# Narrow 0/1 rows of a graph kernel made tile by tile from one source, in rows with gaps

## The chip, the cores and the metric

The kernel runs on one core of a Trainium2 chip. The metric is the device time of one execution in microseconds. Before the change three runs took 2859.52, 2863.18 and 2864.38 us; the median is 2863.18.

The engines are named as in the profile: PE (TensorE, with PEld for its weight loads), DVE (VectorE), ACT (ScalarE), POOL (GpSimd, which here issues the indirect gathers) and SP (which issues most of the other DMAs).

## What is computed

Two graph layers, a last product, a residual and a layer norm, over 12,500 nodes with 256 features and 200,000 edges. `dst` is sorted, and drawn so that small node numbers get many more edges.

```python
def _sage_conv(x, src, dst, W_l, b_l, W_r):
    msgs = x[src]
    agg = jax.ops.segment_sum(msgs, dst, num_segments=N_NODES)
    deg = jax.ops.segment_sum(jnp.ones((src.shape[0],), x.dtype), dst, num_segments=N_NODES)
    mean = agg / jnp.maximum(deg, 1.0)[:, None]
    return mean @ W_l + b_l + x @ W_r
...
h = jax.nn.relu(_sage_conv(x, src, dst, W1_l, b1, W1_r))
h = jax.nn.relu(_sage_conv(h, src, dst, W2_l, b2, W2_r))
return h @ W3 + b3
...
x = _layernorm(x + _L0_gnn_ref(...), axis=-1)
```

## The kernel before

The edges are cut into 1563 tiles of 128. The aggregation is made in two ways, side by side.

**Cold nodes** (few edges each) are gathered. One round takes four tiles: POOL issues four indirect DMAs (`got`, L251), each of which brings 128 rows of `x` or `h`. DVE makes the 0/1 matrix `one` (`select`, L208), PE multiplies it with the rows into `part_ps` (L263), ACT copies this to `some` (L273), DVE makes a second 0/1 matrix `two` (L214: 128 lanes compared with one number per partition, written in f32), PE multiplies again into `sum_ps` (L279, L285), and DVE adds that to a ring of sums (L293) and degrees (L289). There are four `got` buffers, so a gather of round i + 4 needs the products of round i to be done.

**Hot nodes** (the first 5 blocks of 256 nodes in layer 1, 7 in layer 2) are counted. For every block `count` (L669) goes through its tiles of edges and makes, for each tile, the 0/1 rows `pick` (L684: 5, 7 or 9 times 98 elements wide, f16 in, bf16 out), `low` (L688: 128 wide) and, from tile 128 on, `aft` (L694: 98 wide). `low` and `aft` are made for four tiles in one instruction, from two sources that are both spread over the tiles. PE multiplies `low` with `pick` and the `low` of the tile before with its `aft` into `count_ps` (L716 while a tile is below 128, L727 and L731 from there). ACT (L733), or DVE below tile 128 (L720), puts the result into the count matrix of the block. `product` (L645 to L666) then multiplies the counts with all rows of `x` or `h`, which were split into three bf16 parts before (`split_rows`, L640: DVE's `rest` and `parts`, L635 and L636; SP stores them). In layer 2 the counts of four blocks are loaded again instead of made.

Each finished block of 128 nodes goes through `first_block` or `last_block`: the products with W_l and W_r (`sage`, L882 and L887), and DVE's and ACT's work on them.

**What orders the work.** PE's and POOL's orders are as written in the program; the other engines' orders are chosen by a scheduler. `layer` (L576) goes round by round: it issues the next round of gathers, then fills in as much of the counting, products and splits as a table of costs says is due for this round (`count_cost` and its neighbours, L757 to L764), with pieces of finished blocks between. So PE works off a fixed mixture, in which the gathers' products stand between the counting and the dense products. Layer 1 has six stages: the count of block 0 beside the splits, and then the count of the next block beside the product of the one before. Layer 2 follows, with the count of the last block only. Inside `count`, `pick` runs one tile ahead:

```python
for t in range(lo_g, highs[g]):
    for u in (t, t + 1):
        if u < highs[g] and u not in ahead:
            ahead[u] = pick(u)
    r, s, aft = ahead.pop(t)
```

There are three `pick` buffers, and two of `low` and `aft` with four tiles each. The weights of both layers are loaded at the start over ACT's queue (`weight`, L541) into tiles of their own.

Of the kernel before, what the change touches and what calls it, by code (L numbers as in the profile page):

```python
# [7 lines left out]
F32 = mybir.dt.float32  # L8
F16 = mybir.dt.float16
# [14 lines left out]
P = 128  # L24
# [25 lines left out]
def by_runs(  # L50
# [86 lines left out]
    lo_t2 = consts.tile([P, P], BF16, name="lo_t2")  # L137
    lo2 = consts.tile([P, len(groups)], F32, name="lo2")
    place = consts.tile([1, len(groups)], I32, name="place")
    low_t = consts.tile([P, HC * P], BF16, name="low_t")  # L140
    spans = [(lows[g] // P, -(-highs[g] // P)) for g in range(HG)]
    tiles_of = [highs[g] - lows[g] for g in range(HG)]
    key_t = [consts.tile([P, n], F32, name=f"key_t{g}") for g, n in enumerate(tiles_of)]
    after_t = [consts.tile([P, n], F16, name=f"after_t{g}") for g, n in enumerate(tiles_of)]
    offs = [consts.tile([1, n], I32, name=f"offs{g}") for g, n in enumerate(tiles_of)]

    ident = consts.tile([P, P], F32, name="ident")
    lane_b = consts.tile([P, P], BF16, name="lane_b")
    steps = consts.tile([P, WIDEST * NB], F16, name="steps")
    ones = consts.tile([P, 1], F32, name="ones")  # L150
    ones_b = consts.tile([P, 1], BF16, name="ones_b")
    zeros_b = consts.tile([P, P], BF16, name="zeros_b")
# [49 lines left out]
    def select(g, r, second):  # L202

        t0, n = groups[g]
        lo, c0 = (lo_t2, C2) if second and t0 // P == C2 else (lo_t, C0)
        a = t0 - c0 * P + r
        one = chosen_pool.tile([P, G, W], F32, name="one", bufs=AHEAD + 1)
        nc.vector.tensor_tensor(  # L208
            one, lo[:, a:a + n * (G - 1) + 1:n].unsqueeze(2).to_broadcast([P, G, W]),
            lane_b[:, :W].unsqueeze(1).to_broadcast([P, G, W]), op=OP.is_equal)  # L210
        if r < n - 1:
            return one, None
        two = chosen_pool.tile([P, P], F32, name="two", bufs=AHEAD + 2)
        nc.vector.tensor_scalar(two, lane_b, lo2[:, g:g + 1], None, op0=OP.is_equal)  # L214
        return one, two

    def left_after(g):

# [76 lines left out]
    with tc.tile_pool(name="setup", bufs=1) as su, \  # L295
# [58 lines left out]
                       allow_small_or_imprecise_dtypes=True)  # L354
        nc.vector.tensor_scalar(ident, diff, 0.0, None, op0=OP.is_equal)
        nc.vector.tensor_copy(lane_b, lane)


        def columns(t, cs, to, name, t0=0, a=None, b=None):
# [178 lines left out]
                                       accum_out=test(1))  # L538


    def weight(w, name):  # L541
        t = consts.tile([P, NC, w.shape[1]], F32, name=name)
        nc.scalar.dma_start(t, w.rearrange("(c p) f -> p c f", p=P))
        return t

    w1l_sb, w1r_sb = weight(w1l, "w1l_sb"), weight(w1r, "w1r_sb")
    w2l_sb, w2r_sb, w3_sb = weight(w2l, "w2l_sb"), weight(w2r, "w2r_sb"), weight(w3, "w3_sb")

    biases = consts.tile([P, 3, D], F32, name="biases")
    for i, b in enumerate((b1, b2, b3)):  # L550
# [25 lines left out]
    def layer(gathers, block, n_pieces, dense, dense_cost):  # L576


        queue, waiting, done = [], [], set()
        turn = 0  # L580

        def begin():
            if waiting and len(queue) < MOST:
                b, *of = waiting.pop(0)
                p = block(b, *of)
                next(p)
                queue.append([b, p, n_pieces - 1, turn + APART])

        def pieces():


            nonlocal turn
            turn += 1
            q = next((q for q in queue if q[3] <= turn), None)
            if q:
                next(q[1])
                q[2:] = q[2] - 1, turn + APART
                if q[2] == 0:
                    done.add(q[0])
                    queue.remove(q)  # L600
            begin()

        filler = dense(waiting)
        spent = 0.0

        def fill(upto):
            nonlocal spent
            while spent < upto:
                spent += next(filler, 1e9)

        i0, n = gathers.i, len(gathers.rounds)
        begun = gathers.hot // P
        for i in range(i0, n + 1):
            before = gathers.step()
            due = dense_cost * min(1.0, (i + 1 - i0) / (n - i0 - 8))
            for part in range(3):
                if part == 2 and before:
                    gathers.summed(*before, done)
                    while begun < left_after(before[0]):
                        waiting.append((begun,))  # L620
                        begun += 1
                pieces()
                fill(spent + (due - spent) / (3 - part))
        fill(1e8)
        while queue or waiting:
            pieces()
# [42 lines left out]
    def count(g, to):  # L669

        lo_g = lows[g]
        off_dve = Values(offs[g], lo_g, DVE, DN)
        off_act = Values(offs[g], lo_g, ACT, DN)
        n_pick = 0
        ahead = {}
        fours = {}

        def pick(t):
            nonlocal n_pick
            w = room(t)  # L680
            i = n_pick % len(picks)
            r = picks[i]
            n_pick += 1
            nc.vector.tensor_scalar(r[:, :w * NB], steps[:, :w * NB],  # L684
                                    key_t[g][:, t - lo_g:t - lo_g + 1], None, op0=OP.is_equal)
            if t % G == 0:
                low = work.tile([P, G, P], BF16, name="low")
                nc.vector.tensor_tensor(  # L688
                    low, low_t[:, t:t + G].unsqueeze(2).to_broadcast([P, G, P]),
                    lane_b.unsqueeze(1).to_broadcast([P, G, P]), op=OP.is_equal)  # L690
                aft = None
                if t + G >= FIRST:
                    aft = work.tile([P, G, NB], BF16, name="aft")
                    nc.vector.tensor_tensor(  # L694
                        aft, after_t[g][:, t - lo_g:t - lo_g + G].unsqueeze(2).to_broadcast([P, G, NB]),
                        steps[:, :NB].unsqueeze(1).to_broadcast([P, G, NB]), op=OP.is_equal)
                fours[t // G] = low, aft
            low, aft = fours[t // G]
            return r, low[:, t % G], None if aft is None else aft[:, t % G]

        before = None
        for t in range(lo_g, highs[g]):
# [4 lines that stand above are left out]
            w = room(t)  # L707

            halves = [(a, min(a + 5, w)) for a in range(0, w, 5)]
            if t < FIRST:  # L710
                j = t % G
                if j == 0:
                    ps = count_pool.tile([P, 1024], F32, name="count_ps")
                    c = ps[:, 512 - 5 * NB:][:, :w * NB]
                for a, b in halves:
                    nc.tensor.matmul(c[:, a * NB:b * NB], lhsT=s, rhs=r[:, a * NB:b * NB],  # L716
                                     start=j == 0, stop=j == G - 1)
                if j == G - 1:
                    into = to[:, :, bass.ds(off_dve.at(t - j), w)]
                    nc.vector.tensor_tensor(into, into, c.rearrange("p (d s) -> p s d", s=NB), op=OP.add)  # L720
                yield count_cost(t)
            else:
                ps = count_pool.tile([P, 1024], F32, name="count_ps")
                c = ps[:, 512 - 5 * NB:][:, :w * NB]
                for a, b in halves:
                    alone = a > 0 or before is None
                    nc.tensor.matmul(c[:, a * NB:b * NB], lhsT=s, rhs=r[:, a * NB:b * NB],  # L727
                                     start=True, stop=alone)
                    if not alone:

                        nc.tensor.matmul(c[:, :NB], lhsT=before[0], rhs=before[1],  # L731
                                         start=False, stop=True)
                nc.scalar.copy(to[:, :, bass.ds(off_act.at(t), w)], c.rearrange("p (d s) -> p s d", s=NB))  # L733
                yield count_cost(t)
            before = s, aft
            if t == FIRST - 1:

                most = work.tile([P, 1], F32, name="most", bufs=1)
                nc.vector.tensor_reduce(most, to[:, :, :NEAR], axis=mybir.AxisListType.XY, op=OP.max)
                nc.vector.tensor_scalar(test(), most, 256.0, None, op0=OP.is_ge)  # L740
# [231 lines left out]
        layer(gathers_1, first_block, 3, staged(stages_1), cost_of(stages_1))  # L972
    block_pool = ctx.enter_context(tc.tile_pool(name="block_ps", bufs=2, space=PSUM))
    count_pool = ctx.enter_context(tc.tile_pool(name="count_ps", bufs=1, space=PSUM))
    layer(Gathers(h_d, True), last_block, 5, staged(stages_2), cost_of(stages_2))


# [377 lines left out]
```

## Time and profile before

| | |
|---|---|
| median of three runs | 2863.18 us |
| the profiled execution | 2859.81 us |
| its span | 2858.0 us |
| mean granted TensorE clock | 0.92 |
| PE's busy share, by fortieths | `3465768978988998999985777878888898999995` |
| POOL's | `5777887777777777777775777777777777777771` |
| DVE's | `6688775654554565665563124443323343444443` |
| the chain that ended last | PE 45%, DMA 21%, POOL 10%, "issue" 6%, DVE 3%, ACT 2% |

The rows by fortieths give the busy tenths of 71 us each. The gathers of layer 1 run from 24.7 to 1520.6 us and those of layer 2 from 1545.0 on; the step between them can be seen as the 5 in PE's and POOL's rows. In the groups, "xcount | busy, mean ns | idle before" stands behind the names; the releaser behind an idle time says what came last. "issue" means that nothing in the profile was waited for.

### The profile page before, as it was taken

The page shows a single profiled execution, that of the slowest core. Times are in us where ns is not written, and L with a number is a line of the kernel's source. Part 1 is how long each engine was busy: PE and PEld are TensorE (multiplying, and loading weights), DVE is VectorE, ACT ScalarE, POOL GpSimd, SP SyncE. Part 2 cuts the span into 40 slices and gives each one's busy share as a digit, 9 for nine tenths or more (in the row PEclk, how much of TensorE's full clock was granted, in tenths as well). Part 3 has the DMA queues.
Part 4 walks back from the last instruction along what each step waited for, and adds up shares of the span by engine and source line. Part 5 has one row for each costly group of instructions (what it writes and reads, how often), then busy time and mean ns, then how long its engine had stood idle before and what let it go on. Part 6 is the DMA issues. An engine that isn't in the chain of part 4 may idle for free.

```text
span 2858.0 us, 53490 instructions
## 1 busy us (share of the span) xinstructions
PE 2327.7 (81%) x18268; PEld 1602.2 (56%) x18268; DVE 1455.2 (51%) x4334; ACT 1098.8 (38%) x2270; POOL 2092.5 (73%) x2074
## 2 busy tenths in 40 slices
PE   3465768978988998999985777878888898999995
PEld 1122325655755666766764455556566666777773
DVE  6688775654554565665563124443323343444443
ACT  0432765654554564565562013333111122222222
POOL 5777887777777777777775777777777777777771
PEclk9777668999988999999998999899999999999998
DMA  4466669768868869867864777677889889888872
GB/s 124 141 201 208 186 194 304 244 203 284 271 202 283 272 209 306 261 204 246 264 187 146 232 247 223 217 221 242 282 289 304 288 284 305 281 270 267 271 245 64
DMA packets 420974, 676.49 MB, mean 237 GB/s; under 512 B 72419, under 2 KB 279385, under 8 KB 420697
## 3 DMA queue, kind: packets, MB, share of 16 engines
q1 hardware_dynamic: 316263, 400.60, 42.8%
q0 software_dynamic: 99072, 270.66, 30.7%
q8 instruction: 150, 2.46, 0.3%
q10 hardware_dynamic: 5362, 1.72, 0.3%
q14 instruction: 127, 1.04, 0.1%
HBM read 582.84 MB, written 89.92 MB: 235 GB/s over the span
## 4 chain that ended last, share of the span: by engine, by line
PE 45%; DMA 21%; POOL 10%; issue 6%; DVE 3%; ACT 2%; DVEq 0%; SPq 0%; ACTq 0%; POOLq 0%
PE dense_ps L659 17%; POOL got L251 10%; PE part_ps L263 6%; PE block_ps L882 5%; DMA rows<-x_d 5%; DMA rows<-h_d 5%; PE block_ps L887 4%; DMA got<-h_d,src_t 4%; PE count_ps L727 4%; DMA x_sb<-in_x_dram 4%; DMA got<-in_x_dram,src_t 3%; PE sum_ps L279 3%; PE block_ps L954 2%; PE block_ps L859 2%; ACT counts L733 1%
## 5 line engine op out<-in xcount | busy, mean ns | idle before, releaser
L251 POOL DMA_INDIRECT got<-in_x_dram,src_t x1076 | 1143.7, 1063 | 374.1 <-issue 286.6
L251 POOL DMA_INDIRECT got<-h_d,src_t x988 | 946.7, 958 | 336.0 <-issue 261.0
L659 PE MATMUL dense_ps<-counts,rows 128*128 128x256 bf16 x7056 | 951.2, 277 | 86.2 <-DMA rows<-h_d 47.7
L659 PEld LDWEIGHTS <-rows 128*128 128x128 bf16 x7056 | 670.0, 99 | 307.6 <-issue 84.8
L733 ACT CAST counts<-count_ps 128x686 f32 (+2 forms) x620 | 540.3, 872 | 263.5 <-PE count_ps L727 193.3
L263 PE MATMUL part_ps<-got,one 128*32 128x257 f32 (+1 forms) x4128 | 364.5, 427 | 225.0 <-DMA got<-h_d,src_t 107.5
L684 DVE TENSOR_SCALAR pick<-steps,key_t 128x686 bf16<-128x686 f16 (+2 forms) x748 | 300.0, 411 | 134.4 <-PE count_ps L727 114.8
L727 PE MATMUL count_ps<-pick,low 128*128 128x490 bf16 (+2 forms) x1052 | 324.4, 362 | 47.3 <-ACT counts L733 25.9
L208 DVE TENSOR_TENSOR one<-lo_t,lane_b 128x128 f32<-128x128 bf16 x516 | 148.2, 287 | 346.3 <-PE part_ps L263 342.3
L273 ACT COPY some<-part_ps 128x257 f32<-128x257 f32 (+1 forms) x361 | 134.5, 373 | 427.0 <-PE part_ps L263 426.1
L263 PEld LDWEIGHTS part_ps<-got,one 128*32 128x32 f32 x4128 | 87.9, 112 | 343.5 <-issue 281.0
L890 ACT COPY sums<-zero 128x256 f32<-128x256 f32 x172 | 69.4, 404 | 444.1 <-PE block_ps L887 442.5
L279 PE MATMUL sum_ps<-two,some 128*128 128x128 f32 x1444 | 236.7, 289 | 0.8 <-DVE sums L293 0.8
L293 DVE TENSOR_TENSOR sums<-sums,sum_ps 128x256 f32 x361 | 148.3, 411 | 145.6 <-PE sum_ps L279 112.0
L279 PEld LDWEIGHTS sum_ps<-two,some 128*128 128x128 f32 x1444 | 205.3, 201 | 16.9 <-issue 10.0
L893 DVE TENSOR_TENSOR own<-block_ps,biases 128x256 f32<-128x256 f32 x196 | 82.8, 422 | 231.1 <-PE block_ps L887 230.5
L727 PEld LDWEIGHTS <-low 128*128 128x128 bf16 x1052 | 105.3, 101 | 153.8 <-DVE pick L684 49.8
L861 ACT COPY own_t<-block_ps 128x256 f32<-128x256 f32 x294 | 109.0, 372 | 123.5 <-PE block_ps L859 122.6
L688 DVE TENSOR_TENSOR low<-low_t,lane_b 128x512 bf16<-128x512 bf16 x187 | 127.7, 683 | 32.5 <-PE count_ps L731 32.3
L896 ACT ACTIVATE h<-own 128x256 f32<-128x256 f32 x196 | 81.6, 416 | 148.8 <-DVE own L894 142.3
L731 PE MATMUL count_ps<-aft,low 128*128 128x98 bf16 x614 | 134.7, 219 | 0.0
L882 PE MATMUL block_ps<-w1l_sb,sums 128*128 128x256 f32 x352 | 113.3, 450 | 11.0 <-DVE sums L293 5.7
(177 smaller groups left out, 2428.0 us busy)
## 6 DMA issues: line engine op xcount, KB each, us to landing
rows<-h_d SPq DMA_DIRECT2D x343, 384.0 KB
rows<-x_d SPq DMA_DIRECT2D x245, 384.0 KB
count_d<-counts SPq DMA_DIRECT2D x28, 896.0 KB
counts<-count_d SPq DMA_DIRECT2D x28, 896.0 KB
x_sb<-in_x_dram SPq DMA_DIRECT2D x194, 128.0 KB
x_d<-parts SPq DMA_DIRECT2D x98, 192.0 KB
h_d<-parts SPq DMA_DIRECT2D x98, 192.0 KB
got<-in_x_dram,src_t POOLq DMA_INDIRECT x1076
```

Source lines behind the costliest of these rows:

```text
L208: nc.vector.tensor_tensor(one, lo[:, a:a + n * (G - 1) + 1:n].unsqueeze(2).to_broadcast([P, G, W]), lane_b[:, :W].unsqueeze(1).to_broadcas ...
L251: rows = nc.gpsimd.indirect_dma_start(out=g[:, j, :D], out_offset=None, in_=self.table, in_offset=bass.IndirectOffsetOnAxis(ap=src_t[:, e: ...
L263: strip = nc.tensor.matmul(part_ps[j * W:(j + 1) * W, :width], lhsT=one[:, j], rhs=g[:, j, :width], start=r == 0, stop=r == n - 1)
L273: nc.scalar.copy(some[:, :width], part_ps[:, :width])
L279: nc.tensor.matmul(sum_ps[:, c], lhsT=some[:, c * P:(c + 1) * P], rhs=two, start=True, stop=True)
L293: nc.vector.tensor_add(own, own, sum_ps[:, :NC])
L659: nc.tensor.matmul(ps[:, c], lhsT=rows[:, b % 2, k, c * P:(c + 1) * P], rhs=c_sb[:, b, :DN], start=False, stop=b == NB - 1 and k == 2 and ...
L684: nc.vector.tensor_scalar(r[:, :w * NB], steps[:, :w * NB], key_t[g][:, t - lo_g:t - lo_g + 1], None, op0=OP.is_equal)
L727: nc.tensor.matmul(c[:, a * NB:b * NB], lhsT=s, rhs=r[:, a * NB:b * NB], start=True, stop=alone)
L731: nc.tensor.matmul(c[:, :NB], lhsT=before[0], rhs=before[1], start=False, stop=True)
L733: nc.scalar.copy(to[:, :, bass.ds(off_act.at(t), w)], c.rearrange("p (d s) -> p s d", s=NB))
L882: product = nc.tensor.matmul(ps[:, 0], lhsT=agg[:, c], rhs=wl[:, c], start=c == 0, stop=c == NC - 1)
```

## The change

`low`, `aft` and `two` get another form. Two new constants hold the numbers 0, 1, 2, ... in rows with gaps: `lanes_5` has 5 rows of 26, at a distance of 28, and `steps_7` has 7 rows of 14, at a distance of 16. Each narrow 0/1 row is now one `tensor_scalar` for one tile: one source (the rows with gaps) is compared with one f32 number per partition, and the result is written as one run. `low` and `two` are 130 elements wide now, of which 128 are used; `aft` stays at 98. `low` is made 748 times instead of 187, and `aft` 621 times instead of 156; `two` stays at 361. `low` and `aft` have six buffers. `pick` and `one` stay as they were. `low_t` and `after_t`, which hold the numbers to compare with, become f32. To make room, the left weights of both layers share one tile, and so do the right ones: the weights of layer 2 are loaded between the layers, over SP's queue. PE's and POOL's instructions keep their order.

```diff
-    low_t = consts.tile([P, HC * P], BF16, name="low_t")
+    low_t = consts.tile([P, HC * P], F32, name="low_t")
...
-    after_t = [consts.tile([P, n], F16, name=f"after_t{g}") for g, n in enumerate(tiles_of)]
+    after_t = [consts.tile([P, n], F32, name=f"after_t{g}") for g, n in enumerate(tiles_of)]
...
+    LW = 130
+    lanes_5 = consts.tile([P, 5, LW // 5 + 2], F16, name="lanes_5")
+    steps_7 = consts.tile([P, 7, NB // 7 + 2], F16, name="steps_7")
...
-        two = chosen_pool.tile([P, P], F32, name="two", bufs=AHEAD + 2)
-        nc.vector.tensor_scalar(two, lane_b, lo2[:, g:g + 1], None, op0=OP.is_equal)
-        return one, two
+        two = chosen_pool.tile([P, LW], F32, name="two", bufs=AHEAD + 2)
+        nc.vector.tensor_scalar(two.rearrange("p (a b) -> p a b", a=5), lanes_5[:, :, :LW // 5],
+                                lo2[:, g:g + 1], None, op0=OP.is_equal)
+        return one, two[:, :P]
...
+        nc.vector.tensor_copy(lanes_5[:, :, :LW // 5], steps_f[:, :LW].rearrange("p (a b) -> p a b", a=5))
+        nc.vector.tensor_copy(steps_7[:, :, :NB // 7], steps_f[:, :NB].rearrange("p (a b) -> p a b", a=7))
...
-    def weight(w, name):
-        t = consts.tile([P, NC, w.shape[1]], F32, name=name)
-        nc.scalar.dma_start(t, w.rearrange("(c p) f -> p c f", p=P))
+    def weight(w, name, tag, queue=nc.scalar):
+        t = consts.tile([P, NC, w.shape[1]], F32, name=name, tag=tag)
+        queue.dma_start(t, w.rearrange("(c p) f -> p c f", p=P))
...
-            if t % G == 0:
-                low = work.tile([P, G, P], BF16, name="low")
-                nc.vector.tensor_tensor(
-                    low, low_t[:, t:t + G].unsqueeze(2).to_broadcast([P, G, P]),
-                    lane_b.unsqueeze(1).to_broadcast([P, G, P]), op=OP.is_equal)
-                aft = None
-                if t + G >= FIRST:
-                    aft = work.tile([P, G, NB], BF16, name="aft")
-                    nc.vector.tensor_tensor(
-                        aft, after_t[g][:, t - lo_g:t - lo_g + G].unsqueeze(2).to_broadcast([P, G, NB]),
-                        steps[:, :NB].unsqueeze(1).to_broadcast([P, G, NB]), op=OP.is_equal)
-                fours[t // G] = low, aft
-            low, aft = fours[t // G]
-            return r, low[:, t % G], None if aft is None else aft[:, t % G]
+            low = work.tile([P, LW], BF16, name="low", bufs=6)
+            nc.vector.tensor_scalar(low.rearrange("p (a b) -> p a b", a=5), lanes_5[:, :, :LW // 5],
+                                    low_t[:, t:t + 1], None, op0=OP.is_equal)
+            aft = None
+            if t + 1 >= FIRST:
+                aft = work.tile([P, NB], BF16, name="aft", bufs=6)
+                nc.vector.tensor_scalar(aft.rearrange("p (a b) -> p a b", a=7), steps_7[:, :, :NB // 7],
+                                        after_t[g][:, t - lo_g:t - lo_g + 1], None, op0=OP.is_equal)
+            return r, low[:, :P], aft
...
+    w2l_sb, w2r_sb = weight(w2l, "w2l_sb", "wl", nc.sync), weight(w2r, "w2r_sb", "wr", nc.sync)
     layer(Gathers(h_d, True), last_block, 5, staged(stages_2), cost_of(stages_2))
```

More of the change, by code (lines that the diff above doesn't have):

```diff
@@ L143, in by_runs @@
     key_t = [consts.tile([P, n], F32, name=f"key_t{g}") for g, n in enumerate(tiles_of)]
-    after_t = [consts.tile([P, n], F16, name=f"after_t{g}") for g, n in enumerate(tiles_of)]
+    after_t = [consts.tile([P, n], F32, name=f"after_t{g}") for g, n in enumerate(tiles_of)]
     offs = [consts.tile([1, n], I32, name=f"offs{g}") for g, n in enumerate(tiles_of)]
     ident = consts.tile([P, P], F32, name="ident")
+    LW = 130
+    lanes_5 = consts.tile([P, 5, LW // 5 + 2], F16, name="lanes_5")
+    steps_7 = consts.tile([P, 7, NB // 7 + 2], F16, name="steps_7")
+    assert NB % 14 == 0
     lane_b = consts.tile([P, P], BF16, name="lane_b")
@@ L538, in by_runs @@
                                        accum_out=test(1))
-    def weight(w, name):
-        t = consts.tile([P, NC, w.shape[1]], F32, name=name)
-        nc.scalar.dma_start(t, w.rearrange("(c p) f -> p c f", p=P))
-        return t
-    w1l_sb, w1r_sb = weight(w1l, "w1l_sb"), weight(w1r, "w1r_sb")
-    w2l_sb, w2r_sb, w3_sb = weight(w2l, "w2l_sb"), weight(w2r, "w2r_sb"), weight(w3, "w3_sb")
+    def weight(w, name, tag, queue=nc.scalar):
+        t = consts.tile([P, NC, w.shape[1]], F32, name=name, tag=tag)
+        queue.dma_start(t, w.rearrange("(c p) f -> p c f", p=P))
+        return t
+    w1l_sb, w1r_sb = weight(w1l, "w1l_sb", "wl"), weight(w1r, "w1r_sb", "wr")
+    w3_sb = weight(w3, "w3_sb", "w3")
     biases = consts.tile([P, 3, D], F32, name="biases")
@@ L675, in count @@
         ahead = {}
-        fours = {}
         def pick(t):
```

## The prediction, made before the changed kernel was run

> **What bounds the kernel now.** I read the shares first, then POOL's groups, then a table by stage, then the timelines.
>
> ```profile
> PE 2327.7 (81%) x18268; PEld 1602.2 (56%) x18268; DVE 1455.2 (51%) x4334; ACT 1098.8 (38%) x2270; POOL 2092.5 (73%) x2074
> ...
> L251 POOL DMA_INDIRECT got<-in_x_dram,src_t x1076 | 1143.7, 1063 | 374.1 <-issue 286.6
> L251 POOL DMA_INDIRECT got<-h_d,src_t x988 | 946.7, 958 | 336.0 <-issue 261.0
> ```
>
> PE looks like the bound, but POOL's idle time is almost all "issue": about 0.30 us before every gather. The tile view of got has a median gather of 949 ns, so POOL's shortest pitch is 0.949 + 0.304 = 1.253 us. Layer 2: 988 x 1.253 = 1238 us, and its gathers run from 1545.0 to 2803.3 = 1258 us. POOL paces it with 20 us to spare. Layer 1: 1076 x 1.253 = 1348 us, but it takes from 24.7 to 1520.6 = 1496 us. The missing 148 us are gathers over 949 ns (1143.7 - 1076 x 0.949 = 122.6 us) and waits, of which 36.2 for PE.
>
> ```profile
> core 0: us, PE busy (x) PEld busy (x) DVE busy (x) ACT busy (x) POOL busy (x), PEclk, DMA share, GB/s
> 60.00:400.00 340.00, 200.30 (x1007) 85.83 (x1007) 260.21 (x742) 154.57 (x328) 264.00 (x217) 0.74 0.60 181
> 400.00:1000.00 600.00, 513.45 (x4318) 350.50 (x4318) 332.10 (x975) 324.82 (x600) 457.73 (x448) 0.92 0.80 255
> 1000.00:1520.00 520.00, 478.83 (x4220) 342.19 (x4217) 317.15 (x966) 299.70 (x573) 393.36 (x388) 0.97 0.75 238
> ```
>
> Mean gather: 264.00/217 = 1217 ns while DVE is 77% busy, 1022 and 1014 ns at 55% and 61%. PE is at 59%, 86% and 92%: slack for POOL to use early, little late. The timelines show one long gather and DVE over it:
>
> ```profile
> 303.93 4.58 POOL L251 DMA_INDIRECT got<-in_x_dram,src_t  x1 [0.30 <-issue]
> 308.82 0.95 POOL L251 DMA_INDIRECT got<-in_x_dram,src_t  x1 [0.31 <-issue]
> ```
> ```profile
> 303.76 0.67 DVE L688 TENSOR_TENSOR low<-low_t,lane_b 128x512 bf16<-128x512 bf16 x1
> 304.36 0.55 DVE L694 TENSOR_TENSOR aft<-after_t,steps 128x392 bf16<-128x392 f16 x1
> 304.84 0.33 DVE L684 TENSOR_SCALAR pick<-steps,key_t 128x490 bf16<-128x490 f16 x1
> 305.10 0.27 DVE L208 TENSOR_TENSOR one<-lo_t,lane_b 128x128 f32<-128x128 bf16 x1
> 305.30 0.27 DVE L214 TENSOR_SCALAR two<-lane_b,lo 128x128 f32<-128x128 bf16 x1
> ...
> 307.02 0.67 DVE L688 TENSOR_TENSOR low<-low_t,lane_b 128x512 bf16<-128x512 bf16 x1
> 308.17 0.45 DVE L684 TENSOR_SCALAR pick<-steps,key_t 128x490 bf16<-128x490 f16 x1 [0.48 <-PE count_ps L727]
> ```
>
> The gather ends about 0.9 us after DVE's first pause (307.69): it stood still while DVE ran without a gap. It isn't every DVE instruction. Of the 1051 gathers of 60 to 1520 us I looked in the trace at what DVE ran when each began, and took the mean over 949 ns: nothing running (429 gathers) 10 ns; pick (137) 269; low (79) 344; aft (42) 254; two (23) 260; rest (20) 339; one (55) 86; sums, which reads PSUM and one SBUF tile (50), 44.
>
> **Relief on POOL.** That gives low 27.2, aft 10.7, two 6.0: 43.9 of 117.7 us. [...]
>
> Whether the new forms stay off POOL's way the trace can't show. The built program writes one run of 130 (or 98) from 5 (or 7) rows. [...] Upper end: merge back-to-back holders (pick, low, aft, two, one, rest, parts) into chains as at 303.93; without low, aft and two, the time from a gather's start to its chain's end falls by 70%, 0.70 x 117.7 = 82 us. I take 58, nearer the single-holder count: 30 before 400, 17 in 400 to 1000, 11 after.
>
> **DVE's new work.** DVE overlaps neighbours by some 80 ns, so I count start to start: low 0.60 us (303.76 to 304.36), aft 0.48, two 0.20, pick of 490 0.26. Tensor_tensor's slope is (683 - 554)/(512 - 392) = 1.075 ns per element.
>
> ```profile
> L688 DVE TENSOR_TENSOR low<-low_t,lane_b 128x512 bf16<-128x512 bf16 x187 | 127.7, 683 | 32.5 <-PE count_ps L731 32.3
> L684 DVE TENSOR_SCALAR pick<-steps,key_t 128x490 bf16<-128x490 f16 x252 | 85.5, 356 | 22.6 <-PE count_ps L731 14.1 <-PE count_ps L727 7.2 <-PE count_ps L716 0.6
> L684 DVE TENSOR_SCALAR pick<-steps,key_t 128x882 bf16<-128x882 f16 x212 | 98.2, 466 | 48.3 <-PE count_ps L727 46.0
> L694 DVE TENSOR_TENSOR aft<-after_t,steps 128x392 bf16<-128x392 f16 x156 | 86.5, 554 | 0.1
> ```
>
> pick has the new form (one source, a scalar per partition): (466 - 356)/392 = 0.28 ns per element leaves 219 ns fixed, 139 start to start. With pairs (0.54 ns): low 139 + 130 x 0.54 = 0.21, aft 0.19; two at 1.075 ns: 0.28. Sum: low 748 x 0.21 - 187 x 0.60 = +45; aft 621 x 0.19 - 156 x 0.48 = +43; two 361 x 0.08 = +29: +117 us. Bounds: with the fixed part of one (0.20 - 128 x 1.075 = 0.06 us) +14; with low and aft unpaired (0.28 and 0.24) +200. I take +117, pick being the nearest form. DVE idles half the span, which hides it, except in 60 to 400. There 208 narrow lows, 84 afts and 26 twos add about 13 + 6 + 2 = 21: 281 us busy in what I expect to be 322.
>
> **New waits.** PE and its weight loads waited for low 43 us in 54 cases (it came once per four tiles); now low follows pick each tile, 0.2 us later at PE wherever DVE runs just in time. Behind that wait on PE stand the gathers' matmuls, and POOL waits for those (part_ps, 36.2 us in layer 1). Bounds: 0 (six buffers let low run ahead) to 236 tiles x 0.2 = 47 in the first stage. I put it into the conversion below.
>
> **The rest.** PE's and POOL's instruction orders are unchanged. Two setup copies stand ahead of src_t on DVE, for which POOL first waits (21.9 us): 0 to 0.5, taken as 0, as DVE waits for loads there anyway. W2's two 256 KB loads leave ACT's queue at the start (gain 0 to 2) and go to SP, each waiting for layer 1's last use of W1. Queued behind them are the last block's stores of h, for which POOL stands 24.4 us at 1545. Those stores need the same block's products anyway, so the wait costs nothing extra; 512 KB at the mean 237 GB/s is 2.2 us beside them. Taken together +1 (-2 to +4).
>
> **Sum.** Not all relief becomes time; PE must follow. Before 400 DVE fills up: 0.6 x 30 = 18. 400 to 1000, PE 14% idle, half for gathers: 0.75 x 17 = 13. After 1000, PE 92% busy: 0.35 x 11 = 4. Layer 2 has 9 us of long gathers, 3 under low or aft: 1. So -36; +1 for the weights, +3 for later sums and picks on a fuller DVE: -32. The profiled execution took 2859.8 us (span 2858.0), giving 2828; it lies 3.4 under the median 2863.2, so 2831.
>
> **Rivals.** (a) Chains break entirely: 82 us of relief, 0.8 converted: about 2797. For it: gathers of over 4 us lie only over gapless DVE. Against: pick and one remain.
> (b) PE takes over: POOL is freed, but PE at 86 to 92% and rows<-x_d landings set the pace after 400; only about 10 us stay: 2853.
> [...]
> (d) Slower: DVE becomes the bound of 60 to 400. Mechanism: unpaired low and aft and two there add 208 x 0.13 + 84 x 0.12 + 2 = 39, so 299 busy, and DVE's 80 idle us, waits for PE, ACT and split_sb, don't shrink: 379 instead of 340. Less 15 gained later: +24, 2887. It decides once a narrow row costs over about 0.25 us there. DVE's 86% in 200 to 300 us speaks for it, the half-idle DVE elsewhere against.
>
> **Chances.** Forecast (2808 to 2848) 0.48; (a) 0.12; (b) 0.14; (c) 0.10; (d) 0.16. A measurement tells 0.2% (5.7 us) from no change: faster 0.73, same 0.10, slower 0.17. Leaving out the far ends of (a) and (d): 2796 to 2873.
>
> **Signs.** Right: gathers of layer 1 near 1015 ns instead of 1063, none of 4 us over low; low near 290 ns, aft 270, two 355; layer 1's last gather near 1490. Wrong if low takes 350, if PE's idle time before L716 and L727 grows past 80 us, or if gathers stay above 1050.

## The result, and the profile after

The changed kernel takes 2817.20 us (four runs, 2813.32 to 2819.59) where the kernel before takes 2861.35 on the same chip: ratio 0.986 [0.982, 0.991]. The forecast was 2831. The profiled execution took 2817.42 us, with a span of 2815.6: 42.4 us less than before.

The shares and POOL's two groups from the page of the changed kernel (busy us, mean ns of one, idle us before and its largest part):

```profile
PE 2321.8 (82%) x18268; PEld 1594.5 (57%) x18268; DVE 1525.3 (54%) x5362; ACT 1098.5 (39%) x2270; POOL 2014.5 (72%) x2074
...
L257 POOL DMA_INDIRECT got<-in_x_dram,src_t x1076 | 1072.4, 997 | 401.3 <-issue 281.5
L257 POOL DMA_INDIRECT got<-h_d,src_t x988 | 940.0, 951 | 343.7 <-issue 258.7
```

POOL's busy time fell by 78 us, 71.3 of it in layer 1; DVE's rose by 70. PE's is 6 lower, 0.3%. By the tile view of `got`, layer 1's gathers run from 26.8 to 1476.5 us, 1449.7 in place of 1495.9. Layer 2's take 1258.9 in place of 1258.3, the gap between the layers is 24.8 in place of 24.4, and what follows the last gather 55.4 in place of 54.7. So the whole gain, 46 us, was made in layer 1; the later start (26.8 instead of 24.7) and these odds and ends took 4 back. The longest gather is 2.7 us instead of 6.3.

The table by stage of the changed kernel:

```profile
core 0: us, PE busy (x) PEld busy (x) DVE busy (x) ACT busy (x) POOL busy (x), PEclk, DMA share, GB/s
60.00:400.00 340.00, 208.73 (x1041) 84.03 (x1042) 282.06 (x996) 161.56 (x341) 241.29 (x231) 0.78 0.64 189
400.00:1000.00 600.00, 535.03 (x4555) 368.87 (x4554) 371.58 (x1467) 337.26 (x621) 448.85 (x460) 0.93 0.82 265
1000.00:1520.00 520.00, 467.21 (x4079) 333.86 (x4077) 328.21 (x1209) 290.84 (x569) 370.14 (x379) 0.96 0.73 233
```

Read POOL's column by counts. Counted from 60 us, it has made 231 - 217 = 14 gathers more than before by 400 us, worth 17.5 us at a pitch of 1.25; by 1000 us it is 26 more, 33 us; at the end 46 us. The mean gather of the three stages went from 1217, 1022 and 1014 ns to 1045, 976 and 977. On the counts of before that frees 37, 21 and 14 us.

The three new forms, by shape:

```profile
L694 DVE TENSOR_SCALAR low<-lanes,low_t 128x130 bf16<-128x130 f16 x748 | 201.7, 271 | 93.7 <-PE count_ps L733 91.9
L699 DVE TENSOR_SCALAR aft<-steps,after_t 128x98 bf16<-128x98 f16 x621 | 155.9, 251 | 0.0
L219 DVE TENSOR_SCALAR two<-lanes,lo 128x130 f32<-128x130 f16 x361 | 121.2, 336 | 3.8 <-PE sum_ps L291 3.6
```

And the timelines of POOL and of DVE around the time at which before had its 4.58 us gather:

```profile
300.39 1.30 POOL L257 DMA_INDIRECT got<-in_x_dram,src_t  x1 [0.30 <-issue]
302.00 0.95 POOL L257 DMA_INDIRECT got<-in_x_dram,src_t  x1 [0.30 <-issue]
303.25 0.95 POOL L257 DMA_INDIRECT got<-in_x_dram,src_t  x1 [0.30 <-issue]
```
```profile
301.06 0.26 DVE L694 TENSOR_SCALAR low<-lanes,low_t 128x130 bf16<-128x130 f16 x1
301.25 0.24 DVE L699 TENSOR_SCALAR aft<-steps,after_t 128x98 bf16<-128x98 f16 x1
301.42 0.39 DVE L691 TENSOR_SCALAR pick<-steps,key_t 128x490 bf16<-128x490 f16 x1
301.72 0.26 DVE L694 TENSOR_SCALAR low<-lanes,low_t 128x130 bf16<-128x130 f16 x1
...
301.97 0.25 DVE L699 TENSOR_SCALAR aft<-steps,after_t 128x98 bf16<-128x98 f16 x1
...
303.05 0.47 DVE L896 SCALAR_TENSOR_TENSOR own<-block_ps,rdeg,own 128x256 f32<-128x256 f32 x1
```

DVE runs just as gaplessly there, and the gathers go through it. The 1.30 us one began over `one` and met `parts`, `pick`, `low`, `aft` and the next `pick`; it lost 0.35 us. The next began over an `aft` (301.97) and the third over an instruction that reads PSUM (303.05), both without a loss. The same count as in the prediction over the whole trace (what did DVE run when a gather began, and how far over 949 ns was it on average, from 60 us to the end of layer 1):

| running on DVE | before: gathers, ns | after: gathers, ns |
|---|---|---|
| `low` | 80, 378 | 84, 4 |
| `aft` | 42, 254 | 97, 7 |
| `pick` (unchanged) | 137, 269 | 156, 109 |
| `parts` (unchanged) | 51, 98 | 57, 171 |
| `rest` (unchanged) | 20, 339 | 23, 271 |
| all gathers | 117.7 us | 46.8 us |

The prediction's row for `low`, 79 and 344, leaves out one gather: that of 4.00 us at 94.6 us, which also began over a `low`. The rows of `low` and `aft` answer the question that the prediction had to leave open. `pick`'s row is the other news: the same instruction costs a gather 109 instead of 269 ns. The likely reason is that what comes after it no longer holds POOL; the run `tt_tile` below bears this out (217 ns again).

### The profile page after: what moved, and what is told of

The parts are those of the page before. It is cut to its first block, busy times and chain, and to the rows that moved or that the text cites. A ratio compares the mean times of both kernels' runs of the same rounds, so it can differ in the third digit from the quotient of the medians.

```text
span 2815.6 us, 54531 instructions
## 1 busy us (share of the span) xinstructions
PE 2321.8 (82%) x18268; PEld 1594.5 (57%) x18268; DVE 1525.3 (54%) x5362; ACT 1098.5 (39%) x2270; POOL 2014.5 (72%) x2074
## 5 line engine op out<-in xcount | busy, mean ns | idle before, releaser
L257 POOL DMA_INDIRECT got<-in_x_dram,src_t x1076 | 1072.4, 997 | 401.3 <-issue 281.5
L257 POOL DMA_INDIRECT got<-h_d,src_t x988 | 940.0, 951 | 343.7 <-issue 258.7
L729 PE MATMUL count_ps<-pick,low 128*128 128x490 bf16 (+2 forms) x1052 | 320.8, 358 | 57.7 <-DVE low L694 32.0
L694 DVE TENSOR_SCALAR low<-lanes,low_t 128x130 bf16<-128x130 f16 x748 | 201.7, 271 | 93.7 <-PE count_ps L733 91.9
L699 DVE TENSOR_SCALAR aft<-steps,after_t 128x98 bf16<-128x98 f16 x621 | 155.9, 251 | 0.0
```

The costliest lines, as they stand in the source:

```text
L257: rows = nc.gpsimd.indirect_dma_start(out=g[:, j, :D], out_offset=None, in_=self.table, in_offset=bass.IndirectOffsetOnAxis(ap=src_t[:, e: ...
L694: nc.vector.tensor_scalar(low.rearrange("p (a b) -> p a b", a=5), lanes_5[:, :, :LW // 5], low_t[:, t:t + 1], None, op0=OP.is_equal)
L699: nc.vector.tensor_scalar(aft.rearrange("p (a b) -> p a b", a=7), steps_7[:, :, :NB // 7], after_t[g][:, t - lo_g:t - lo_g + 1], None, op0 ...
```

## The experiments

That the gain is POOL's the result shows. Open was what let POOL through: the single source of `low`, `aft` and `two`, the rows with gaps, or that the instructions are short and for one tile each; the moved weights could also have a part. The expectations call "port theory" the account that certain DVE instructions keep POOL's gather from ending while they run; "port" is the author's name for it, and no run shows what the two engines would share. Which instructions these are changed on the way: before `flat` they were thought to be those whose rows have no gaps (the strong form), with the single source on the rival's side; from `tt_tile` on those with a second source. Twelve runs were made. They fell on three chips, and on two of these the kernel before takes 3361 to 3368 us instead of 2858, so each is set against the kernel before on its own chip. On those slower chips POOL does not set the pace. In `weights_only`, which is before but for the loads, it stands 155 us waiting for PE's `part_ps` in layer 1 where the kernel before stood 36:

```profile
POOL got L251 <- PE part_ps L263: 36.2, 40, 5.0
```
```profile
L251 POOL DMA_INDIRECT got<-in_x_dram,src_t x1076 | 1137.3, 1057 | 625.9 <-issue 268.6 <-PE part_ps L263 154.7 <-remote 62.3
```

The length of a gather can be read there, its worth in time only as POOL's share of the pace allows. Why these chips are slower was not found: the mean granted clock is 0.88 there against 0.92, and of the 502 us that the span is longer PE is busy for 192 and idle for 310.

**The weights alone.** Before, with only the edit of the loads:

```diff
+    w2l_sb, w2r_sb = weight(w2l, "w2l_sb", "wl", nc.sync), weight(w2r, "w2r_sb", "wr", nc.sync)
```

> The kernel before, with only the weights of layer 2 moved behind layer 1 in shared tiles. My account (the weights cost nothing): the same as before within 3 us, and the same 24 us between the last gather of layer 1 and the first of layer 2. Rival (the moved loads, or the start without them, are part of the gain or hide part of it): a difference of 5 us or more.

Measured: 3361.82 us, ratio 1.0005 [0.998, 1.003], mean gather of layer 1 1057 ns (1063 on before's page). The weights do nothing that can be measured there, within 0.3%.

**One row at a time.** `low_only` has the new `low` with the old `aft` and `two`; `aft_only` the new `aft` alone.

> The changed kernel with only low in the new form; aft (four tiles at once) and two as before. Port theory with single holders: low's share, 27 of 44 us of the relief, so gathers of layer 1 near 1020 ns and 2835 to 2840. Port theory with chains: less than its share, since aft follows low on DVE and keeps POOL out: near 1035 ns and 2842 to 2850. Rival (DVE bound in the first stage): PE's waits for low are there without most of the relief, and the time is 2855 or more.

> The changed kernel with only aft in the new form; low (four tiles at once) and two as before. Single holders: 11 of 44 us of the relief, 2848 to 2853. Chains: 2853 to 2860, as low stands ahead of aft and holds by itself. Rival (DVE's extra time alone decides): 2861 or more.

Measured: 3353.78 us, 0.9967 [0.995, 0.999], gather 1005 ns; and 3351.67 us, 0.9962 [0.993, 0.999], 1025 ns. In time they can't be told apart. In the gathers `low` alone gives 52 ns, more than expected, and `aft` alone 32, against `weights_only` on the same chip. The whole change gives 68 by the same measure (`after_b`, below, on the other slow chip), less than 52 + 32: the reliefs don't add. This fits chains of holders that `low` alone already breaks, but no run isolates it.

**Rows without gaps.** `flat` is the changed kernel with the same instructions from plain sources:

```diff
-            nc.vector.tensor_scalar(low.rearrange("p (a b) -> p a b", a=5), lanes_5[:, :, :LW // 5],
-                                    low_t[:, t:t + 1], None, op0=OP.is_equal)
+            nc.vector.tensor_scalar(low, lanes_f, low_t[:, t:t + 1], None, op0=OP.is_equal)
```

It was run on all three chips (`flat`, `flat_b` on the faster one, `flat_c`).

> The changed kernel, but the sources of low, aft and two lie as one run without gaps (130 or 98 numbers): as many instructions, one source each, only the row pattern differs. [...] Rival (what helped is that the instructions became short, or have one source): low falls to about 255 ns, DVE gets some 60 us lighter, gathers stay at 1000 ns or less and the time is 2817 or less.

> The flat sources again (low, aft and two without gaps), on another chip if there is one: on the first, PE lost so much time waiting for nothing the profile shows that POOL did not set the time. There the mean gather of layer 1 was 1004 ns with flat sources, against 1057 with the old forms, so my port theory in its strong form is in doubt. Port theory, weak form (gaps are worth something, short instructions most): mean 1000 to 1010 ns, 2818 to 2832 us. Strong form: 1040 or more and 2845 or more. Rival (short instructions are all of it): 2817 or less, since DVE is lighter.

> Flat sources on the same chip as the changed kernel. From the two profiles: gathers of layer 1 are 5 ns longer (5 us over 1076) and DVE is as heavy once its own waits for POOL are counted. Gaps worth what the profiles say: 5 to 10 us slower than the changed kernel. Rival (one source is all of it): within 3 us.

Measured: 3350.57 us, 0.9967 [0.994, 0.999]; 2829.21, 0.9902 [0.987, 0.994]; 3342.38, 0.9962 [0.993, 0.999]. Mean gathers 1004, 1002 and 1007 ns. The page's line of `flat_b`:

```profile
L255 POOL DMA_INDIRECT got<-in_x_dram,src_t x1076 | 1078.1, 1002 | 408.6 <-issue 283.4
```

So without any gaps the gathers stay 50 to 61 ns below before's (1057 and 1063), and the port theory in its strong form, with 1040 ns or more, is refuted. The changed kernel has 5 ns less (997 against 1002) on the faster kind of chip, and 18 less (989 against 1007) on the third. The price is on DVE: in `flat_b` a `low` has a median of 252 ns, but a tenth of them take 370 or more, up to 500. With a plain source it is DVE's instructions that get longer. Layer 1's gathers run 1461.5 us there, 12 longer than in the changed kernel. The changed kernel's ratio was not measured beside it, and the intervals overlap; on the third chip, side by side, the two can't be told apart (below). The gaps may be worth 12 us, but the runs don't show it in time.

**Tile by tile with two sources.** `tt_tile` keeps the short instructions, and makes `low` and `aft` from two sources again:

```diff
+            nc.vector.tensor_tensor(low[:, :P], low_t[:, t:t + 1].to_broadcast([P, P]), lane_b, op=OP.is_equal)
...
+                nc.vector.tensor_tensor(aft, after_t[g][:, t - lo_g:t - lo_g + 1].to_broadcast([P, NB]),
+                                        steps[:, :NB], op=OP.is_equal)
```

> low and aft made tile by tile, but each still as tensor_tensor from two sources, about as long as the new form (128 elements one by one); two as in the changed kernel. Rival (being short is what counts, not the number of sources): gathers that begin under low or aft lose as little as in flat, under 100 ns, and 2815 to 2830. Port theory (two sources shut POOL out for the rest of their length): they lose 120 to 200 ns each, but there is less length to lose, mean gather 1015 to 1030, 2825 to 2842.

Measured: 2874.04 us, ratio 1.0061 [1.004, 1.009]: slower than before, and slower than either expectation had it. `low` takes 282 ns and `aft` 250, nearly as in the changed kernel (271, 251). It is POOL that differs. Its group in `tt_tile`, then one gather and DVE beside it from the timelines:

```profile
L257 POOL DMA_INDIRECT got<-in_x_dram,src_t x1076 | 1134.2, 1054 | 391.7 <-issue 284.0
```
```profile
276.41 4.50 POOL L257 DMA_INDIRECT got<-in_x_dram,src_t  x1 [0.30 <-issue]
```
```profile
277.25 0.27 DVE L694 TENSOR_TENSOR low<-low_t,lane_b 128x128 bf16<-128x128 bf16 x1
277.45 0.38 DVE L691 TENSOR_SCALAR pick<-steps,key_t 128x686 bf16<-128x686 f16 x1
277.76 0.40 DVE L644 TENSOR_TENSOR parts<-rest 128x256 bf16<-128x256 f32 x1
278.10 0.41 DVE L643 TENSOR_TENSOR rest<-split_sb 128x256 f32<-128x256 f32 x1
278.43 0.27 DVE L694 TENSOR_TENSOR low<-low_t,lane_b 128x128 bf16<-128x128 bf16 x1
```

The long gathers are back (up to 6.9 us), over the same mixture on DVE with only the form of `low` and `aft` changed. This is the sharpest of the runs: same count, nearly the same length, same place, one more source, and 1054 instead of 997 ns (1032 without the six gathers of over 4 us). With the second source come another operation, `tensor_tensor`, and numbers to compare with in bf16 and f16; these were not taken apart. Of the gathers, the 102 that begin over a `low` lose 271 ns again, the 81 over an `aft` only 58, and the unchanged `pick` costs its 147 gathers 217 ns on average instead of 109, so what runs around it counts.

**The forms by themselves.** `streams` is not the kernel's computation: 24 gathers run beside a stream of one form at a time on DVE, and the output is a copy of `x`.

> Not the computation: seven stretches, each with 24 gathers of 128 rows on POOL beside one form of DVE instruction run back to back (none; low's old form for four tiles, two sources, 512; the same from two sources for one tile, 128; one source without gaps, 130; one source in rows with gaps, 130; pick's form without gaps, 686; and with gaps, 686). The output is a copy of x. Theory A (an instruction with two sources keeps POOL out for as long as DVE finds the next one; one with one source lets POOL in at its end; one in rows with gaps never keeps it out): with two sources a gather lasts several us or until the stream ends, whether 512 or 128 long; one source without gaps 1000 to 1300 ns, and DVE's own instructions stretch; with gaps 946 ns. Theory B (every holder keeps POOL out for the rest of one instruction only): 128 from two sources at most 1150 ns, 512 up to 1500, and the same for one source of the same length.

Measured, from POOL's groups by shape (`long` is two sources and 512 elements, `short` two sources and 128, `run` one source without gaps, `gaps` with, `wide` a 686 wide one without):

```profile
L87 POOL DMA_INDIRECT got<-in_x_dram,at_short x24 | 58.7, 2445 | 14.8 <-DVE made_short L64 7.8 <-issue 7.0
L87 POOL DMA_INDIRECT got<-in_x_dram,at_wide x24 | 23.7, 986 | 25.8 <-DVE at_wide L85 18.8 <-issue 7.0
L87 POOL DMA_INDIRECT got<-in_x_dram,at_long x24 | 22.9, 956 | 9.3 <-issue 9.3
L87 POOL DMA_INDIRECT got<-in_x_dram,at_run x24 | 22.8, 951 | 9.3 <-issue 7.0 <-DVE made_run L67 2.3
L87 POOL DMA_INDIRECT got<-in_x_dram,at_gaps x24 | 22.7, 948 | 31.3 <-DVE made_gaps L70 24.3 <-issue 7.0
```
```profile
112.78 36.45 DVE L64 TENSOR_TENSOR made_short<-key_b,lane_b 128x128 bf16<-128x128 bf16 x180
113.13 36.92 POOL L87 DMA_INDIRECT got<-in_x_dram,at_short  x1 [7.84 <-DVE made_short L64]
150.36 0.95 POOL L87 DMA_INDIRECT got<-in_x_dram,at_short  x1 [0.30 <-issue]
```

The mean of 2445 ns is one gather of 36.92 us and 23 of 0.95. The one that began inside the stream of 180 short two-source instructions ended 0.8 us after the last of them (149.23), as the prediction's long gather ended 0.8 us after DVE's pause (308.51 and 307.69). It is one gather in one run. Narrow rows of one source cost next to nothing: with gaps the first twelve gathers, under an unbroken stream, took 942 to 949 ns, without gaps the first four 945 to 993. Later in both streams DVE pauses, for a reason that the profile doesn't show, so the other gathers test less. Wide rows without gaps cost some 30 ns a gather, wide ones with gaps none (at most 950). Of the narrow rows with gaps none was stretched (longest 283 ns), without gaps up to 495. That is theory A's case.

The `long` row goes against it: two sources, and only the first gather was late (1147 ns, as was the first one with no stream, 1093). There every later gather began 0 to 7 ns after a DVE instruction began. POOL had fallen into step with DVE, and each gather went through in the stretch that it always met. In the kernel, where `low` of 512 stood in a mixture, 80 gathers met it and lost 378 ns on average. Why an even stream lets POOL in and the mixture doesn't is not settled.

**Longer DVE rows, POOL free.** `unpaired` is the changed kernel with its two sources in f32:

```diff
-    lanes_5 = consts.tile([P, 5, LW // 5 + 2], F16, name="lanes_5")
-    steps_7 = consts.tile([P, 7, NB // 7 + 2], F16, name="steps_7")
+    lanes_5 = consts.tile([P, 5, LW // 5 + 2], F32, name="lanes_5")
+    steps_7 = consts.tile([P, 7, NB // 7 + 2], F32, name="steps_7")
```

> [...] My account (DVE is nearly the bound of the first stage): the 400 us mark is reached with 6 to 12 fewer gathers, 2822 to 2835. Rival (DVE has slack everywhere): no change within 4 us, 2814 to 2821.

Measured: 2843.06 us, 0.9945 [0.992, 0.997], 8 us above the highest time expected. `low` takes 337 ns and `aft` 301, against 271 and 251 in the changed kernel, and the gathers are as free as ever (995 ns against 997). From its page, and the waits of POOL in layer 1 (us in total, times, longest), its own and then the changed kernel's:

```profile
L257 POOL DMA_INDIRECT got<-in_x_dram,src_t x1076 | 1070.5, 995 | 434.0 <-issue 276.4
```
```profile
POOL got L257 <- PE part_ps L269: 103.0, 67, 11.0
```
```profile
POOL got L257 <- PE part_ps L269: 59.8, 45, 9.7
```

POOL waits 103 us for PE's products, against 60 in the changed kernel. DVE is busy 56 us longer between 60 and 1520 us, and layer 1's gathers take 1481.1 us, 31 more: 0.56 us for each us of DVE's. So length on DVE isn't free in layer 1 although DVE idles a third of it: it comes out at PE, and from there at POOL.

**More relief.** `pick_later` takes the largest remaining holder too: from the second block on, `pick` is made from rows with gaps (and `aft` has five buffers instead of six, to make room).

```diff
+                nc.vector.tensor_scalar(r[:, :w * NB].rearrange("p (a b) -> p a b", a=w), steps_g[:, :w, :NB],
+                                        key_t[g][:, t - lo_g:t - lo_g + 1], None, op0=OP.is_equal)
```

> The changed kernel with the picks too from rows with gaps, from the second block of nodes on (the first stage, where DVE is full, keeps the wide form); aft has five buffers for room. DVE gets some 520 x 0.19 = 100 us more between 400 and 2000, where it is half to two thirds busy. Port theory: gathers that begin under pick stop losing their 110 ns, 13 us of relief in layer 1, of which half is time: 2806 to 2815. Rival (DVE and the path from pick to PE decide): PE waits longer for pick, 2820 to 2840.

Measured: 2826.38 us, 0.9881 [0.982, 0.994], so no better than the changed kernel, as the rival had it. Its page and its waits of POOL:

```profile
L258 POOL DMA_INDIRECT got<-in_x_dram,src_t x1076 | 1059.8, 985 | 424.8 <-issue 281.3
```
```profile
POOL got L258 <- PE part_ps L270: 88.8, 62, 11.0
```

The gathers give 12.6 us more, and POOL's wait for PE grows by 29: a 686 wide `pick` now has a median of 559 ns instead of 393.

**The changed kernel where POOL is not the pace.** `after_b` is the changed kernel, `two_old` the same with the old `two`, both beside `flat_c` on the third chip.

> The changed kernel once more, beside flat sources and the old form of two on one chip. All theories: 0.984 to 0.989 of the kernel before.

> The changed kernel with two in its old form (flat, 280 instead of 336 ns). DVE's length counts (the unpaired kernel gave back 26 us for some 70 us of DVE): 361 x 0.055 = 20 us less of DVE is worth 5 to 8 us, against 3 us of relief given up: 2 to 6 us faster than the changed kernel. [...]

Measured: 3345.61 us, 0.9966 [0.994, 0.999], and 3344.25, 0.9958 [0.994, 0.998]. The first expectation, 0.984 to 0.989 by all theories, failed. The page's line of `after_b`:

```profile
L257 POOL DMA_INDIRECT got<-in_x_dram,src_t x1076 | 1063.7, 989 | 686.8 <-issue 261.7 <-PE part_ps L269 213.9 <-remote 69.7
```

The gathers are as much shorter as elsewhere (989 and 998 ns), but POOL now waits 214 us for `part_ps` in layer 1, and the gain is 0.3% instead of 1.4%. Read afterwards, this is a counter-check that nobody had planned: the same relief, without POOL as the pace, is worth a quarter. Whether the new form of `two` helps in time is not to be seen; the gathers are 10 ns longer without it.

## Why the prediction was right, point by point

- **POOL paces the kernel: right.** The gain is in layer 1's gathers, and `after_b` shows what is left of it where POOL isn't the pace. The half on layer 2 was too simple: its gathers got 6.7 us shorter (946.7 to 940.0), and POOL's idle time there grew by 7.7 (336.0 to 343.7; 8.6 of it is waiting for `part_ps`, 16.1 to 24.7), so nothing was left, where I had 1 us.
- **What `low` and `aft` cost POOL: the rows were right.** The rows said 344 ns (378 with the gather left out) and 254, and in the changed kernel 4 and 7 are left. In `tt_tile` the short two-source forms brought `low`'s back (271 ns), `aft`'s only in small part (58 ns); the 36.92 us gather shows the same form by itself. Why a second source makes the gather wait, and which read or write of it waits, no run shows.
- **Relief on POOL: 58 forecast, 71 measured** (by stage 30, 17 and 11 against 37, 21 and 14). I stayed near the count of single holders, 43.9 (46.9 with the gather that the row of `low` leaves out). The term missed is the unchanged `pick`: 137 x 269 = 37 us before, 156 x 109 = 17 after. The upper end, 82, had it by merging holders into chains; the measured value lies halfway between 58 and 82. So rival (a) was half at work. About 3 of the 71 us are not relief, but an undisturbed gather of 946 instead of 949 ns.
- **"Whether the new forms stay off POOL's way": they do, and the gaps have little part in it.** `flat_b` has no gaps, and its gathers take 1002 ns, against 997 in the changed kernel and 1063 before. The one source did most of it: with two, in `tt_tile`, they take 1054. What the rows with gaps did is on DVE: none stretched (longest `low` 284 ns, against 500 in `flat_b`). With f16 numbers a `low` takes 271 ns, with f32 337 (`unpaired`).
- **DVE's new work: +117 forecast, +70 measured.** From `low` to `aft` 0.19 us pass, from `aft` to the next instruction 0.17, and after a `two` 0.26, where I had 0.21, 0.19 and 0.28: 30 + 31 + 22 = 83 in place of 117. The other 13 are `pick`'s, whose part of DVE's busy time fell from 264 to 251 us. No run shows the 0.54 ns per element of "with pairs"; it was an assumption, half of `tensor_tensor`'s 1.075. Between `aft` and `low`, 32 elements apart, the runs show (271 - 251)/32 = 0.63 ns with f16 and, in `unpaired`, (337 - 301)/32 = 1.13 with f32. At 0.63 the fixed part of a narrow row is 0.11 us start to start, some 0.03 less than the 0.139 estimated from `pick`. (The lower bound of the working, +14, does not follow from its own terms: with a fixed part of 0.06 us they give 748 x 0.13 - 187 x 0.60 = -15 and 621 x 0.113 - 156 x 0.48 = -5, so about -20.)
- **Conversion: 0.60 forecast, 46/71 = 0.65 measured, with errors inside it.** From 60 to 400 us it was 17.5/37 = 0.47 instead of 0.60, then 15/21 instead of 0.75, and after 1000 us 13/14 instead of 0.35. "PE 92% busy" was a poor reason for 0.35: PE went to 99.6% between 1100 and 1200, and stood 30 us further in its work at 1000 already. A share of 92% was still 8% of slack, 41 us of 520, more than the 14 asked for.
- **New waits: as foreseen, and (d) partly there.** PE's waits for `pick` and `low` together were 63 us before and 84 after, now nearly all for `low`. Of these 57 lie between 100 and 300 us, and POOL's wait for `part_ps` rose from 12.6 to 33.4 between 60 and 400: the part of the relief that (d) took. Its point lay too low, and its place was too narrow: in `unpaired` a `low` is at 0.19 + 0.066 = 0.256 us, past the 0.25 that I gave, and the kernel keeps 0.55% of the 1.38%; and DVE's extra length there is 3 us before 400 and 53 after.
- **Signs.** Layer 1's mean gather 997 (1015 forecast), none over 4 us, `low` 271 (290), `aft` 251 (270), `two` 336 (355), last gather 1475.5 (1490): all on the right side, the forms each some 19 ns short. The sign of 80 us of PE idle before L716 and L727 was ill set: it was 53.9 + 47.3 = 101 before already, and is 57.1 + 57.7 = 115 after.
- **Weights and start.** Nothing measurable for the weights, by `weights_only`; the gap between the layers did not grow. The first gather began 2.1 us later, where I had up to 0.5.

The miss of the middle, 42.4 us of span against 32, is thus mostly the 13 us of extra relief from broken chains, some 8 us at 0.65, and a last stage that turned nearly all of its relief into time; cheaper DVE rows went the same way, and a later start the other.

The profile lines behind the new waits, PE's products of `pick` and `low` and their weight loads in the changed kernel:

```profile
L729 PE MATMUL count_ps<-pick,low 128*128 128x490 bf16 (+2 forms) x1052 | 320.8, 358 | 57.7 <-DVE low L694 32.0
L729 PEld LDWEIGHTS <-low 128*128 128x128 bf16 x1052 | 104.3, 100 | 159.4 <-DVE low L694 61.5
```

Before, the same two were led by "ACT counts" and "DVE pick". `low`, made after `pick`, is now what PE is late for.

## What to carry to other kernels

If POOL issues the gathers and paces the kernel, sort the gathers by what DVE runs when they begin: the rows say which DVE form holds them, and an instruction made from one source instead of two may give back more than its own row (here 71 us, where the rows of `low`, `aft` and `two` had 46.9). Then watch DVE's length in the same stage: relief for POOL bought with longer rows on DVE (`unpaired`, `pick_later`) returned as POOL's wait for PE (103.0 and 88.8 us against 59.8). And ask first whether that engine is the pace on the chip at hand: the same relief was worth 1.4% where POOL was, and 0.3% where it was not.

## What was not expected of the hardware

- A stream of 180 short two-source instructions (277 ns each, one every 202 ns) kept a single gather from ending for 36.92 us, from its start to 0.8 us after the stream's end; 60 instructions of 512 elements (697 ns, one every 621) delayed at most the first (1147 ns; the first one with no stream took 1093).
- With one source and no gaps it is DVE that gives way: 260 ns rows stretched to 495, and 401 ns ones to 606, while gathers lost 4 and 39 ns at the mean (951 and 986, over a median of 947 with no stream). Only the first four gathers of the narrow stream stood under it without a pause; they took 945 to 993.
- The same kernel took 2858 us on one chip and 3361 to 3368 on two others, with POOL waiting for PE there; the cause was not found.
